# 491 counted edge tiles in place of 363 in a two-layer graph kernel, with the order inside a step changed

## The chip, the cores and the metric

The kernel runs on one core of one Trainium2 chip. The time is device time in microseconds, the median of several runs; a profile shows one execution. The engines are named as in the profile: PE is TensorE (PEld its weight loads), DVE VectorE, ACT ScalarE, POOL GpSimd, SP the engine that issues most plain DMAs.

## The reference

Two graph layers over 12500 nodes of 32 features and 200000 edges, which are sorted by their destination `dst`:

```python
h = jnp.maximum(_layernorm(x, axis=-1), 0.0)
x = x + _L0_gnn_ref(h, L0_gnn_W, L0_gnn_b, src, dst)
h = jnp.maximum(_layernorm(x, axis=-1), 0.0)
x = x + _L1_gnn_ref(h, edge_index, edge_attr_4, W1, b1, W2, b2, W3, b3, W4, b4)
```

The first layer sums over edges and scales by degrees:

```python
out_norm = jax.lax.rsqrt(jnp.maximum(out_deg, 1.0))
in_norm = jax.lax.rsqrt(jnp.maximum(in_deg, 1.0))
h = x * out_norm[:, None]
agg = jax.ops.segment_sum(h[src], dst, num_segments=N_NODES)
out = agg * in_norm[:, None] @ W + b
```

The second makes a message for every edge, `relu` layers of 64, 128 and 64 over `[x_i, x_j - x_i] @ W1`, sums the messages by `dst`, and divides by the in-degree. The edge attributes are not used.

## The kernel before

**Edges.** 1563 tiles (`NTR`) of 128 edges, four tiles to a chunk (391 chunks, `NCH`). Because `dst` is sorted, the edges of a chunk fall into a window of 128 nodes, and the windows of following chunks lie 32 nodes apart. A sum over the edges of a tile is a matmul: the gathered rows as weights, a one-hot of (destination minus window) as the moving operand. Rows are split into three bf16 terms, so that a row has 3 x 32 + 1 columns (`D3` = 97, the last one for the degree).

**First stretch (0 to about 340 us in the profile).** Layer norm of x; out-degrees by one-hot matmuls over all tiles; the table `tab_hn` of scaled rows is written to DRAM. Beside it POOL gathers the unscaled rows of the first 64 chunks (`EARLY`) from `tab_h` and from x, one indirect DMA for a tile of 128 edges (line 211).

**Second stretch (about 340 to 1534 us), the sums of layer 0.** Three kinds of chunks make the sums:

- Early chunks (0 to 63): rows are there already; `scale_rows` finds each edge's factor by a look-up matmul (`look`, line 664) and a mask (line 671), scales the rows (679), splits them into three bf16 terms (copies on ACT, lines 682 and 685; subtractions on DVE, line 687), makes a one-hot (`hot_e`), and sums them (line 693). The generator yields between stages; a new chunk starts at every third step.
- Direct chunks (64 to `DIR` - 1 = 299): POOL gathers their scaled rows from `tab_hn`, four gathers a chunk. `sum_rows` does the matmuls (line 628) into `ps_late`, one PSUM bank, of which four chunks share one group; `add_rows` adds the group to the SBUF sums. Eight buffers hold the gathered rows.
- Counted tiles (all from chunk `DIR` on, `ND` = 363 tiles): nothing is gathered. With source node = 128 x high + low, a tile makes a matrix that counts its edges by (low) x (high, destination in the tile's window of 13): three matmuls (line 775, `count_two` and `count_third`) of a one-hot of low (`lo`) with a one-hot of the key (`oh`, line 713, made for two tiles at once), evicted by two ACT copies (line 777). PSUM has one buffer for each. For a group of eight tiles (`TD`), `multiply` then multiplies the counts by the whole table, held in SBUF, in 98 matmuls (line 724), turns the result (733), places it (743) and adds it (`sums.add`, lines 550 and 552: ACT copies fresh columns, DVE adds to others).

When all chunks that reach a block group of four blocks of 128 nodes (25 groups) are added, `update_nodes` is queued for it: in-degree, W0, residual, layer norm, and two tables, `tab_i` and `tab_j`, written for layer 1. It is a generator in six parts; `in_turn` runs one update at a time, one part for each call.

**The order of work.** The second stretch is one Python loop over chunks, and the engines take their instructions in that order (`manual_schedule`). A step of the loop issues, in this order: the four gathers of chunk m; the one-hot (`hot`) of chunk m + 2; the counting stages due (four stages a tile, spread evenly over the steps); one stage of each running early chunk (`advance`); one part of an update; the start of an early chunk; `add_rows` of chunk m - 3; `sum_rows` of chunk m - 2 (`LAG` = 2). After the loop the rest of the counting and of the updates is issued.

**Third stretch (1534 us to the end), the messages.** POOL gathers rows of `tab_j`, one gather a tile, 1563 in all; it can start when the whole table is written. Four layers and the sums run behind it, and `finish_nodes` writes the output. A last branch handles inputs whose windows do not fit; with these inputs it is not entered.

## Time and profile before

| | us |
|---|---|
| median of 3 runs (3518.82 to 3520.71) | 3519.95 |
| the profiled execution | 3515.0 |
| its span | 3513.1 |
| gathers of the first stretch, 256, first and last start | 6.0, 338.0 |
| row gathers of the second, 944, first and last start | 339.3, 1517.2 |
| gathers of the third, 1563, first and last start | 1534.3, 3484.1 |

The page cuts the span into 40 slices of 87.8 us. A digit is the busy share in tenths, PEclk the granted TensorE clock in tenths; the second stretch is slices 4 to 17:

```profile
PE   3762767777777777547777777777777777777777
...
DVE  8994666556666664213333333333333333333333
ACT  0002555455555555201221222112122121221211
POOL 7777777777777777767777777777777777777775
PEclk9655788778889887658887888887888788887888
```

In rows of groups, the first number after the bar is the busy time of all, the second the mean of one in ns, then the idle time of the engine ahead of them and what ended it. "Issue" is time in which the engine waited for nothing that the profile shows.

### The profile page before, as it was taken

To read this page: it belongs to the slowest core of one execution; us is meant where nothing else is said; L and a number is where in the kernel's file an instruction comes from. 1 tells how busy PE (TensorE), PEld (TensorE's weight loads), DVE (VectorE), ACT (ScalarE), POOL (GpSimd) and SP (SyncE) were. 2 spreads that over 40 slices of the span, in tenths; PEclk is the share of its full clock that TensorE was granted. 3 is DMA by queue.
4 is the path that set the end of the run, shared out by engine and by line. 5 is a ranking of instruction groups with operands and counts; after the bars stand their busy time and mean duration, and the time that the engine had idled before them with its cause. 6 is when DMAs were issued, how large, how long until landed. Compare 5 with 4: busy or idle time off the path is not lost. (4 is left out here: it accounts for less than half of the span.)

```text
span 3513.1 us, 50240 instructions
## 1 busy us (share of the span) xinstructions
PE 2465.8 (70%) x18988; PEld 1733.6 (49%) x18988; DVE 1654.0 (47%) x3694; ACT 1016.1 (29%) x2052; POOL 2622.9 (75%) x2783
## 2 busy tenths in 40 slices
PE   3762767777777777547777777777777777777777
PEld 2650545555555555424445544445544444444445
DVE  8994666556666664213333333333333333333333
ACT  0002555455555555201221222112122121221211
POOL 7777777777777777767777777777777777777775
PEclk9655788778889887658887888887888788887888
DMA  4114111212222211212222222222222222222221
GB/s 94 15 20 72 28 27 30 37 30 38 34 32 36 34 28 30 44 42 59 62 62 61 61 58 61 61 62 58 61 62 61 61 59 61 62 61 61 60 60 31
DMA packets 238466, 173.58 MB, mean 49 GB/s; under 512 B 157810, under 2 KB 186706, under 8 KB 238218
## 3 DMA queue, kind: packets, MB, share of 16 engines
q0 software_dynamic: 88416, 79.14, 14.2%
q1 hardware_dynamic: 131306, 85.26, 8.9%
q10 hardware_dynamic: 18496, 5.89, 1.1%
q8 instruction: 154, 2.52, 0.3%
q14 instruction: 94, 0.77, 0.1%
HBM read 157.16 MB, written 12.92 MB: 48 GB/s over the span
## 5 line engine op out<-in xcount | busy, mean ns | idle before, releaser
L211 POOL DMA_INDIRECT gj<-tab_j,src_j x1563 | 1474.7, 944 | 492.1 <-issue 422.1
L211 POOL DMA_INDIRECT rows<-tab_hn,src_j x944 | 891.5, 944 | 287.7 <-issue 218.8
L916 DVE TENSOR_TENSOR h<-p,b3n 128x512 f32<-128x512 f32 x196 | 135.2, 690 | 731.7 <-PE p L913 731.7
L913 PE MATMUL p<-w3s,h 128*128 128x64 f32 x3128 | 435.5, 298 | 0.3 <-ACT h L905 0.3
L913 PEld LDWEIGHTS p<-w3s,h 128*128 128x128 f32 x3128 | 407.9, 211 | 47.3 <-issue 38.2
L777 ACT ACTIVATE count<-count_two 128x858 bf16<-128x858 f32 x363 | 320.9, 884 | 366.3 <-PE count_two L775 340.1
L881 PE MATMUL p<-gj,ident 128*1 128x8 f32 x392 | 39.1, 175 | 530.1 <-DMA gj<-tab_j,src_j 530.1
L905 ACT ACTIVATE h<-p,b2s 128x1024 f32<-128x1024 f32 x196 | 217.8, 1111 | 641.8 <-PE p L903 641.8
L881 PEld LDWEIGHTS p<-gj,ident 128*1 128x1 f32 x392 | 21.9, 80 | 697.2 <-issue 686.7
L724 PE MATMUL st<-count,table 128*128 128x104 bf16 (+1 forms) x4508 | 333.3, 231 | 35.6 <-ACT count L777 31.9
L931 PEld LDWEIGHTS ps<-hot,h 128*64 128x64 f32 x3126 | 268.9, 188 | 175.0 <-issue 165.3
L724 PEld LDWEIGHTS <-table 128*128 128x128 bf16 x4508 | 304.1, 108 | 103.6 <-issue 67.0
L893 ACT ACTIVATE h<-p 128x512 f32<-128x512 f32 x196 | 117.0, 597 | 810.5 <-PE p L889 810.5
L889 PE MATMUL p<-turned,ai 128*64 128x512 f32 x782 | 327.2, 928 | 0.0
L552 DVE TENSOR_TENSOR acc<-acc,ps 64x64 f32<-64x64 f32 (+1 forms) x198 | 44.7, 226 | 534.1 <-PE ps L931 501.4
L931 PE MATMUL ps<-hot,h 128*64 128x128 f32 x3126 | 293.7, 349 | 0.5 <-DVE h L916 0.5
L775 PE MATMUL count_two<-oh,lo 128*128 128x429 bf16 x726 | 240.5, 418 | 51.6 <-ACT count L777 40.7
L713 DVE TENSOR_TENSOR oh<-keys,kept 128x2574 bf16<-128x2574 f16 x182 | 270.4, 1486 | 13.2 <-PE count_third L775 13.0
L211 POOL DMA_INDIRECT rows_early<-tab_h,src_j x224 | 216.2, 965 | 70.3 <-issue 47.2
L865 DVE TENSOR_TENSOR turned<-row,kept 128x512 f32<-128x512 f16 x391 | 249.4, 678 | 26.9 <-PE p L889 22.1
L575 DVE TENSOR_TENSOR hot<-rel_h,kept 128x512 f32<-128x512 f16 x391 | 249.1, 678 | 0.0
L628 PE MATMUL ps_late<-hot,rows 128*97 128x128 bf16 x944 | 135.0, 254 | 161.9 <-DMA rows<-tab_hn,src_j 89.5
(201 smaller groups left out, 3102.2 us busy)
## 6 DMA issues: line engine op xcount, KB each, us to landing
row<-rel_row SPq DMA_DIRECT2D x195, 256.0 KB
gj<-tab_j,src_j POOLq DMA_INDIRECT x1563
rows<-tab_hn,src_j POOLq DMA_INDIRECT x944
ai<-tab_i SPq DMA_DIRECT2D x195, 64.0 KB
srow<-hi_row SPq DMA_DIRECT2D x64, 98.0 KB
rows_early<-tab_h,src_j POOLq DMA_INDIRECT x224
tab_j<-nu_aij SPq DMA_DIRECT2D x24, 128.0 KB
tab_i<-nu_aij SPq DMA_DIRECT2D x24, 128.0 KB
```

Of the source, the lines that this page charges most:

```text
L211: nc.gpsimd.indirect_dma_start(out=tile_ap, out_offset=None, in_=table, in_offset=bass.IndirectOffsetOnAxis(ap=col, axis=0))
L575: nc.vector.tensor_tensor(hot, rel_h[:, g * TPC : (g + 1) * TPC][:, :, None].to_broadcast([P, TPC, W]), lanes_f[:, None, :W].to_broadcast( ...
L713: nc.vector.tensor_tensor(oh, keys[:, :, i : i + 2][:, :, None, :].to_broadcast([P, 3, KW, 2]), count_h[:, None, :, :].to_broadcast([P, 3, ...
L724: nc.tensor.matmul(ps[:, : tiles * WD], table[:, h, :], c[:, :tiles, h, :], start=(h == 0), stop=(h == PART - 1))
L775: nc.tensor.matmul(ps[:, k, :w], lo[:, i % TPC // 2, :, i % 2], oh[:, k0 + k, :w, i % 2], start=True, stop=True)
L777: nc.scalar.activation(counts[g][:, t, a:b, :].rearrange("p (k h) d -> p k (h d)", k=len(ranges)), ps[:, :, :w], AF.Copy)
L865: nc.vector.tensor_tensor(turned, v["row"][:, k], part_f.to_broadcast([P, CHUNK]), op=OP.is_equal)
L889: nc.tensor.matmul(p1[k * HID : (k + 1) * HID].rearrange("p t e -> p (t e)"), v["ai"][:, k], v["turned"][k], start=False, stop=True, skip_ ...
L905: nc.scalar.activation(h2[:, :n], p2[:, :n], AF.Relu, bias=b2s)
L913: nc.tensor.matmul(p3[:, k * TPC + t, :], v["h2"][:, k, t * P : (t + 1) * P], w3s, start=True, stop=True)
L916: nc.vector.tensor_tensor(h3[:, :n], p3[:, :n], b3n[:, None, :].to_broadcast([P, n, HID]), op=OP.max)
L931: nc.tensor.matmul(ps[k * HID : (k + 1) * HID, o : o + W], v["h3"][:, k * TPC + t, :], v["hot"][k][:, t, :], start=(i == 0 and t == 0), st ...
```

## The change

- `DIR` is 268 in place of 300: 32 chunks (128 tiles) go from the direct to the counted kind. `ND` becomes 491, the groups of eight 62 in place of 46, direct chunks 204 in place of 236.
- `multiply` does its 98 products in 5 stages (n = 8 - 3) in place of 18, and a tile of counting takes one stage in place of three. The last products, the copy `some` and the mask `place` are one stage; the transpose comes in the next, the placing matmul two stages on. A tile is one call of the counting generator in place of four.
- A step has a new order: sums first (early chunks' sums, kept in a list `adds`, and `add_rows`), then a part of an update, then counting, then the stages of early chunks, and `sum_rows` last.
- The early rows are split on DVE alone (`memset`, `tensor_copy`) in place of copies on ACT.
- `hot` has 5 buffers in place of 6, `oh` 4 in place of 3; one-hots are made four tiles ahead in place of two.
- `base`, `base8` and `win_i` move to a pool that is freed after the first stretch.

```diff
-DIR = 300
+DIR = 268
@@ hot_ahead
-            hots[g] = one_hots(sp, rel_h[:, g * TPC : (g + 1) * TPC], W, "hot", AHEAD + 4)
+            hots[g] = one_hots(sp, rel_h[:, g * TPC : (g + 1) * TPC], W, "hot", AHEAD + 3)
@@ scale_rows
-            nc.scalar.activation(rows[:, :, 3 * D :], rows_early[:, g, :, D:], AF.Copy)
+            nc.vector.memset(rows[:, :, 3 * D :], 1.0)
             for k in range(3):
                 part = rows[:, :, k * D : (k + 1) * D]
-                nc.scalar.activation(part, scaled, AF.Copy)
+                nc.vector.tensor_copy(part, scaled)
...
+            adds.append((g, total))
             yield
-            sums.add(slice(0, D3), STEP * g, total)
-            added([g])
@@ onehots_of
-            onehots[i // 2] = oh = dp.tile([P, 3, KW, 2], BF16, name="oh", bufs=3)
+            onehots[i // 2] = oh = dp.tile([P, 3, KW, 2], BF16, name="oh", bufs=4)
@@ multiply
-            n = 3 * TD - 6
+            n = TD - 3
             for s in range(n):
...
-                yield
+                if s < n - 1:
+                    yield
...
             nc.scalar.activation(some[:, : tiles * WD], ps[:D3, : tiles * WD], AF.Copy)
+            width = STEP * (GD - 1) + W
+            place = dp.tile([WD * TD, width], F32, name="place")
+            nc.vector.tensor_scalar(
+                place, count_h[: WD * TD, :width, 0], pos[:, g : g + 1], None, op0=OP.is_equal)
             yield
             ps = pp.tile([P, P + STEP], F32, name="st2")
             nc.tensor.transpose(ps[: WD * TD, :D3], some, ident[:D3, :D3])
             turned = dp.tile([WD * TD, D3], F32, name="some_t")
             nc.scalar.activation(turned, ps[: WD * TD, :D3], AF.Copy)
-            width = STEP * (GD - 1) + W
-            place = dp.tile([WD * TD, width], F32, name="place")
-            nc.vector.tensor_scalar(
-                place, count_h[: WD * TD, :width, 0], pos[:, g : g + 1], None, op0=OP.is_equal)
-            yield
             yield
@@ count_edges
             onehots_of(0)
+            onehots_of(2)
...
-                if i % 2 == 0 and i + 2 < ND:
-                    onehots_of(i + 2)
+                if i % 2 == 0 and i + 4 < ND:
+                    onehots_of(i + 4)
                 oh, lo = onehots[i // 2], los[i // TPC]
-                for _ in range(3):
-                    next(before, None)
-                    yield
+                next(before, None)
@@ the loop
-        steps, stages = DIR - EARLY - 6, 4 * (ND + 2 * TD)
+        steps, stages = DIR - EARLY - 6, ND + 2 * TD
...
             i = m - EARLY
+
+            while adds:
+                early, total = adds.pop()
+                sums.add(slice(0, D3), STEP * early, total)
+                added([early])
+            if EARLY <= m - LAG - 1:
+                add_rows(m - LAG - 1)
+            next(updating)
             for _ in range(stages * i // steps, stages * (i + 1) // steps):
                 next(counting, None)
             advance(running)
-            next(updating)
             later, r = divmod(i, LATER)
             if r == 0 and later < EARLY:
                 running.append(scale_rows(later))
-            if EARLY <= m - LAG - 1:
-                add_rows(m - LAG - 1)
             if EARLY <= m - LAG < DIR:
                 sum_rows(m - LAG)
```

More of the change, by code (lines that the diff above doesn't have):

```diff
@@ L146, in gnn_kernel @@
     pos = early.tile([WD * TD, NDG], F32, name="pos")
-    base = early.tile([1, ND], I32, name="base")
-    base8 = early.tile([TD, NDG], I32, name="base8")
     bounds = early.tile([P, 4], F32, name="bounds")
@@ L154, in gnn_kernel @@
     dst_i = mp.tile([P, NT], I32, name="dst_i")
+    base = mp.tile([1, ND], I32, name="base")
+    base8 = mp.tile([TD, NDG], I32, name="base8")
     first = ctx.enter_context(ExitStack())
@@ L172, in gnn_kernel @@
     nc.gpsimd.iota(lanes_i, pattern=[[1, P]], base=0, channel_multiplier=0)
-    win_i = const.tile([P, NCH], I32, name="win_i")
+    win_i = mp.tile([P, NCH], I32, name="win_i")
     nc.gpsimd.iota(win_i, pattern=[[STEP, NCH]], base=-OFF, channel_multiplier=0)
@@ L594, in gnn_kernel @@
         sums = Sums(np_, D3, "acc", (QE, QD, NQ - 1), (QE, QD), lambda q: ("_e", 2) if q < QE else ("_t", 3) if q < QD else ("_d", 3))
-        hots, rows_of, group_ps, running, updates = {}, {}, {}, [], []
+        hots, rows_of, group_ps, running, updates, adds = {}, {}, {}, [], [], []
         updating = in_turn(updates)
```

## The prediction

> **What bounds the kernel now.** I read the page first, then the kernel in three stretches, then who waits for whom in the middle of the second stretch, then single moments of its timeline.

> ```profile
> span 3513.1 us, 50240 instructions
> PE 2465.8 (70%) x18988; PEld 1733.6 (49%) x18988; DVE 1654.0 (47%) x3694; ACT 1016.1 (29%) x2052; POOL 2622.9 (75%) x2783
> ...
> L211 POOL DMA_INDIRECT gj<-tab_j,src_j x1563 | 1474.7, 944 | 492.1 <-issue 422.1
> L211 POOL DMA_INDIRECT rows<-tab_hn,src_j x944 | 891.5, 944 | 287.7 <-issue 218.8
> ```

> POOL issues 2763 gathers of one edge tile each (1563 + 944 + 224 + 32). One takes 944 ns and the idle time ahead of it is about 0.30 us of plain "issue", so 75% busy is a full queue. By the tile view the 944 row gathers start from 339.3 to 1517.2 us: 1177.9 / 943 = 1.249 us each, 4.996 us for the four of a step. The largest distance between two starts there is 1.36 us, so nothing ever holds POOL in the second stretch. It stands still once only, from the last row gather to the first message gather:

> ```profile
> 1517.22 0.94 POOL L211 DMA_INDIRECT rows<-tab_hn,src_j  x1 [0.30 <-issue]
> ...
> 1519.72 1.82 PEld L474 LDWEIGHTS nu_ps<-w0t,acc 97*128 97x128 f32 x8
> ...
> 1529.71 0.60 ACT L511 ACTIVATE nu_aij<-nu_ps 128x512 f32<-128x512 f32 x1 [2.16 <-PE nu_ps L509]
> ...
> 1534.26 0.94 POOL L211 DMA_INDIRECT gj<-tab_j,src_j  x1 [16.09 <-DMA row<-rel_row]
> ```

> That is 17.0 us: 2.5 us until the last row is in a sum, 10.6 us (1519.7 to 1530.3) for one update of nodes, 4.0 us for its store and the release.

> The other engines have less room than their shares say. This is the view by windows (length, then busy time and instructions of PE, weight loads, DVE, ACT, POOL, the granted clock), and the waits of PE in the same window (total, times, longest), then one of DVE's:

> ```profile
> 600.00:1300.00 700.00, 517.72 (x5232) 398.81 (x5231) 444.04 (x1276) 388.75 (x901) 529.09 (x561) 0.83 0.21 34
> ```

> ```profile
> PE ps_late L628 <- ACT acc_t L550: 49.1, 23, 4.0
> PE st L733 <- ACT some L730: 41.6, 24, 5.2
> PE look L664 <- ACT acc_e L550: 38.7, 39, 2.0
> PE count_two L775 <- ACT count L777: 23.9, 19, 3.9
> PE st L724 <- ACT count L777: 18.1, 22, 2.5
> ...
> PE ps_late L628 <- DMA rows<-tab_hn,src_j: 2.7, 3, 1.1
> ```

> ```profile
> DVE look L687 <- ACT rows_scaled L685: 91.3, 92, 6.1
> ```

> The reader is to see the last PE row: in 700 us PE waited for gathered rows 2.7 us. From each gather's start to the matmul of the same tile it is 2.5 us where PE waits, and 8 to 20 us through most of this window, so PE with its waits needs about the same 5.0 us a step as POOL. The window has 140.1 steps: PE is busy 3.70 us and idle 1.30 us in each, and 129.4 of the 182 idle us (0.92 a step) are three waits on ACT copies that stand behind count evictions.

> **Part by part.** POOL: DIR from 300 to 268 takes away 32 chunks, 128 gathers: 128 x 1.249 = 159.9 us. The last of 816 row gathers would start at 339.3 + 815 x 1.249 = 1357.3 us. The message stretch (1563 gathers) stays.

> Counting: 363 tiles become 491, over 192 steps of the loop in place of 221: 2.56 a step against 1.64, so 0.914 more. At full clock a product group of 16 takes 1.00 us, at half clock 1.55 us:

> ```profile
> 806.02 1.55 PE L724 MATMUL st<-count,table 128*128 128x104 bf16 x16 [2.54 <-ACT count L777]
> ...
> 809.02 1.00 PE L724 MATMUL st<-count,table 128*128 128x104 bf16 x16
> ```

> One tile has 98/8 = 12.25 products: 0.64 us at the 52 ns from start to start, 0.77 us by the row above; its three count matmuls start within 0.57 us (809.86 to 810.43). With its share of transpose and placing, 1.3 to 1.4 us: 1.25 us a step. Today's 3.70 us at a mean clock of 0.83 (0.66 of the time full) is 3.70 x (0.66 + 0.34 x 0.65) = 3.26 us at full clock. New: 4.5 us a step.

> DVE: today 444.0 / 140.1 = 3.17 us a step. A tile adds half an L713 (0.743) and a quarter of a L614 (0.103): 0.77 us a step, placing and sums 0.05. The early chunks' three copies: [...] at most 299 (L687, same shape with two inputs); I take 270. With a memset of 60 to 200 ns, 0.1 taken, it is 0.91 us a chunk, one chunk in three steps: 0.3. Sum 4.3 of 5.0 us. For that L687 no longer waits for ACT, 0.65 us a step of DVE's time.

> ACT: 2.77 us a step, plus 0.914 x (0.884 + 0.513) = 1.28, plus 0.1, less the copies (3 x 0.281 + 0.224) / 3 = 0.36: 3.8 us. Two tiles' evictions back to back start 1.52 us apart (1001.06 and 1002.58), and PSUM has one buffer for them: 2.56 x 1.52 = 3.9 us, under a step.

> The order: with the sums first, the ACT copy that frees ps_late or the look bank is issued ahead of the step's evictions, and PE needs the bank at the step's end; the transpose now comes a whole tile after its copy to "some". All three waits (0.92 us a step) should go. What is late next is PE behind count evictions: L775 and L724 (42 us, 0.30 a step) grow at least with the tiles, and each product group's first matmul needs the last tile's two evictions. I take the remaining 0.38 us of idle times 1.56: 0.6. The bounds are 0.3 (denser filling) and 1.2 (a group start at 1.4 us for each of 62 groups and 0.4 us in each of three tiles of eight without products). The update's stage moves ahead of counting with its matmuls, vector work and, in its last stage, two stores on SP; the early chunk's row load is now queued behind these. A row is needed a step later, so I cost that at nothing[...].

> With hot at 5 buffers, hot for chunk m + 2 waits for the matmul of chunk m - 3, the end of PE's step before. Behind it on DVE are the step's sums, update and one-hots. The one-hots run four tiles ahead (oh at 4 buffers), so PE has its input. Taken at nothing; the slower rival prices it.

> PE's step: if denser work raises the clock to 0.95, 4.5 us take 4.5 / 0.965 = 4.65 us, plus 0.6 = 5.25 us against POOL's 5.0. Counting ends at step 197 of 206, the nine after it hold about 11 us of PE work. PE's end: 197 x 5.25 + 11 = 1045 us against 204 x 4.996 = 1019: 26 us late. POOL may be held a little on the way when its eight row buffers are full; the end is PE's all the same.

> The tail: an update takes six calls, one a step. Following the loop's counters, before, only block group 18 was left when the loop ended. After, groups 3, 4 and 15 come due at steps 194 and 195, group 24 at 196 and group 16 at 206; the loop ends with group 4 at its first stage. So three updates follow the last row: 2 x 10.6 = 21 us more. Cover: none, POOL needs the whole table. The first stretch gets five vector instructions 128 columns longer, under 1 us, hidden by the early gathers. The tiles that change their pool cost nothing.

> Sum: -160 + 21 + 26 = -113 us. Against the profiled execution's 3515.0 that is 3402 us; against the median 3519.95, 3407 us.

> **Rivals.** (1) POOL stays the bound: PE's step at 5.16 us or less, with waits of 0.5 us. For: the three waits were 71% of PE's idle time. Against: PE had no room before. Time 3520 - 160 + 21 = 3381 us. (2) The clock does not rise: 4.5 / 0.88 = 5.1 us plus 0.6 = 5.7 us a step, 115 us late: 3520 - 160 + 21 + 115 = 3496 us. For: PE at 74% busy in the message stretch has 0.82. Against: the gaps that let it fall are the ones that go. (3) Slower: DVE and PE in turn. DVE may start a step only when PE has ended the one before (hot, and the sums that wait for PE's last matmuls); if PE then waits within the step for "place" or for the acc_d sum that frees st, DVE's 4.3 us no longer lie beside PE's. From 5.82 us a step on (0.57 over my 5.25) the gain is gone: (1019 + 139 - 11) / 197. With 0.8 us of such waits a step, 6.05 us: 184 us late, 3565 us. For: DVE at 86%. Against: it works four tiles ahead.

> **Numbers.** Forecast 0.47, POOL bound 0.20, clock 0.18, slower 0.15. The range 3374 to 3506 us holds the first three with about 7 us to spare and leaves the fourth out. No change is what this kernel's runs cannot tell apart, 0.2%, 7 us: faster 0.83, same 0.03, slower 0.14.

> **What would show it.** Right: 816 row gathers, the first message gather near 1420 us, three updates in a row ahead of it, acc_t, "some" and acc_e gone from PE's waits, clock over 0.9 between 350 and 1300, PE waiting mostly for count evictions. Wrong: POOL held by ps_late matmuls for long, PE waiting for DVE within a step, the clock still near 0.83, or PE waiting for rows all along (rival 1).

## The result: 0.3% faster, and the profile after

| | before | after |
|---|---|---|
| median of 8 runs each, us | 3519.36 (3518.17 to 3523.34) | 3509.32 (3508.15 to 3514.82) |
| ratio, 95% interval | | 0.9973 (0.9962 to 0.9984) |
| profiled span, us | 3513.1 | 3508.2 |
| first, last row gather | 339.3, 1517.2 | 338.1, 1489.0 |
| first message gather | 1534.3 | 1525.7 |

The forecast was 3407 us and the range ended at 3506. The kernel is faster, but by 10 us and not by 113. The page of the kernel after:

```profile
span 3508.2 us, 54111 instructions
PE 2569.0 (73%) x20860; PEld 1819.5 (52%) x20860; DVE 1807.6 (52%) x4040; ACT 1140.6 (33%) x2092; POOL 2504.7 (71%) x2655
...
POOL 7777777666665666647777777777777777777775
PEclk9755999889898998857887878888887787878778
...
L211 POOL DMA_INDIRECT rows<-tab_hn,src_j x816 | 771.9, 946 | 380.2 <-issue 203.5
```

POOL's row of tenths is no longer flat: from slice 7 on (the first slice is number 0) it is at 6, once at 5, where it was at 7. The 816 gathers should have taken 816 x 1.249 us; their idle time, 380.2 us, is 131 us over the 0.305 us that each had before (287.7 us for 944). That is where the time went: the last row gather starts at 1489.0 us and not at 1357.3, 131.7 us late. From it to the first message gather it is 36.7 us in place of 17.0. So -159.9 + 131.7 + 19.7 = -8.5 us, which is the difference of the two first message gathers.

The same 600 us window in the middle, by windows (length, busy time and instructions of PE, weight loads, DVE, ACT, POOL, clock), and who waited there (total, times, longest):

```profile
600.00:1200.00 600.00, 472.89 (x5132) 363.36 (x5131) 423.51 (x1149) 371.60 (x726) 382.50 (x405) 0.89 0.18 29
```

```profile
PE count_two L773 <- ACT count L775: 57.4, 73, 3.5
PE st L723 <- ACT count L775: 44.2, 25, 4.5
...
PE st L737 <- ACT some L730: 2.6, 2, 2.3
```

```profile
DVE hot L614 <- PE ps_late L628: 155.9, 58, 5.3
```

The same row in the kernel before, in the 700 us from 600 to 1300 us:

```profile
DVE hot L614 <- PE ps_late L628: 5.8, 9, 1.3
```

And in the kernel after again, from 600 to 1200 us, POOL's wait and the matmuls of the direct chunks (name, count, shortest, median and longest in ns, first and last start):

```profile
POOL rows L211 <- PE ps_late L628: 104.3, 53, 5.1
```

```profile
L628 PE MATMUL ps_late<-hot,rows x396: 217/218/314, 600.0 to 1197.5; 128*97 128x128 bf16 x198
```

396 matmuls are the chunks of 99 steps, so a step of PE takes 6.06 us. (POOL's 405 gathers are 101 steps: it runs ahead of PE as far as its eight row buffers go, so gathers do not count PE's steps.) PE is busy 4.78 us of a step, where 4.65 was forecast, and idle 1.28 us, where 0.6 was forecast. The three waits that the new order was to remove are gone (ps_late and look on ACT; "some" from 41.6 us of 700 to 2.6 of 600). In their place PE waits for count evictions, 101.6 us (42.0 of 700 before); POOL waits for the row buffers that PE has not read; and DVE has one wait that it hardly had before, 155.9 us, or about 1.6 us a step, at the one-hot that opens each step.

The chain from that wait to PE can be read at a single moment of the timeline (start, length, instruction, idle time ahead of it and what ended it; a few rows are left out):

```profile
908.58 0.40 PE L628 MATMUL ps_late<-hot,rows 128*97 128x128 bf16 x4
...
909.01 0.42 DVE L614 TENSOR_TENSOR hot<-rel_h,kept 128x512 bf16<-128x512 f16 x1 [2.86 <-PE ps_late L628]
...
909.82 0.55 PE L773 MATMUL count_two<-oh,lo 128*128 128x429 bf16 x2
...
910.84 0.29 DVE L492 TENSOR_TENSOR nu_h<-x,nu_m 128x128 f32<-128x128 f32 x1
911.16 0.31 ACT L493 ACTIVATE nu_t<-nu_h 128x128 f32<-128x128 f32 x1 [1.98 <-DVE nu_h L492]
...
912.09 0.20 ACT L496 ACTIVATE nu_g<-nu_m 128x4 f32<-128x4 f32 x1 [0.62 <-DVE nu_m L495]
912.20 0.87 ACT L775 ACTIVATE count<-count_two 128x858 bf16<-128x858 f32 x1
...
913.12 0.55 PE L773 MATMUL count_two<-oh,lo 128*128 128x429 bf16 x2 [1.51 <-ACT count L775]
```

At 908.58 PE does the last matmuls of a step. DVE has stood still 2.86 us for them, because its next instruction is the one-hot, whose buffer they free. Behind it in DVE's queue is the update's arithmetic, to 911.1; ACT's square (L493) waits 1.98 us for that; and the eviction of counts that PE had ready at 910.4 stands in ACT's queue behind the square and behind a second small instruction of the update (L496), which waits 0.62 us for DVE in its turn, until 912.20. PE, with one PSUM buffer for the counts, then waits 1.51 us. In the whole window PE waits for DVE directly hardly at all: the rows of PE's waits that name DVE come to 4.3 us of 127.

### The profile page after: what moved, and what is told of

It is laid out like the page before. It is cut to its first block, busy times and chain, and to the rows that moved or that the text cites. A ratio compares the mean times of both kernels' runs of the same rounds, so it can differ in the third digit from the quotient of the medians.

```text
span 3508.2 us, 54111 instructions
## 1 busy us (share of the span) xinstructions
PE 2569.0 (73%) x20860; PEld 1819.5 (52%) x20860; DVE 1807.6 (52%) x4040; ACT 1140.6 (33%) x2092; POOL 2504.7 (71%) x2655
## 5 line engine op out<-in xcount | busy, mean ns | idle before, releaser
L211 POOL DMA_INDIRECT gj<-tab_j,src_j x1563 | 1478.0, 946 | 512.0 <-issue 423.8
L211 POOL DMA_INDIRECT rows<-tab_hn,src_j x816 | 771.9, 946 | 380.2 <-issue 203.5
L775 ACT ACTIVATE count<-count_two 128x858 bf16<-128x858 f32 x491 | 434.5, 885 | 261.2 <-PE count_two L773 230.1
L723 PE MATMUL st<-count,table 128*128 128x104 bf16 (+1 forms) x6076 | 393.4, 223 | 67.2 <-ACT count L775 64.6
L723 PEld LDWEIGHTS <-table 128*128 128x128 bf16 x6076 | 367.4, 103 | 116.4 <-issue 48.3
L773 PE MATMUL count_two<-oh,lo 128*128 128x429 bf16 x982 | 294.7, 384 | 128.3 <-ACT count L775 118.2
L712 DVE TENSOR_TENSOR oh<-keys,kept 128x2574 bf16<-128x2574 f16 x246 | 364.9, 1487 | 3.6 <-PE count_third L773 3.6
L211 POOL DMA_INDIRECT rows_early<-tab_h,src_j x224 | 215.6, 963 | 71.5 <-issue 49.4
L773 PEld LDWEIGHTS <-lo 128*128 128x128 bf16 x1473 | 140.5, 105 | 222.9 <-issue 169.2
L775 ACT ACTIVATE count<-count_third 128x416 bf16<-128x416 f32 x491 | 251.6, 512 | 0.0
```

Of the source, the lines that this page charges most:

```text
L211: nc.gpsimd.indirect_dma_start(out=tile_ap, out_offset=None, in_=table, in_offset=bass.IndirectOffsetOnAxis(ap=col, axis=0))
L712: nc.vector.tensor_tensor(oh, keys[:, :, i : i + 2][:, :, None, :].to_broadcast([P, 3, KW, 2]), count_h[:, None, :, :].to_broadcast([P, 3, ...
L723: nc.tensor.matmul(ps[:, : tiles * WD], table[:, h, :], c[:, :tiles, h, :], start=(h == 0), stop=(h == PART - 1))
L773: nc.tensor.matmul(ps[:, k, :w], lo[:, i % TPC // 2, :, i % 2], oh[:, k0 + k, :w, i % 2], start=True, stop=True)
L775: nc.scalar.activation(counts[g][:, t, a:b, :].rearrange("p (k h) d -> p k (h d)", k=len(ranges)), ps[:, :, :w], AF.Copy)
```

## Experiments

Two theories for the 1.28 us of idle time. **H**: the wait of the one-hot holds DVE, DVE's work behind it holds ACT, ACT's evictions hold PE. **E**: the two evictions and their one PSUM buffer are the pace, whatever DVE does. **U**, a part of H: the place of the update ahead of counting is the cost. Ratios are against the kernel before, run beside each. The expectations count steps by POOL's gathers (1.26 us idle, 1.54 us of waiting and 5.95 us a step in the changed kernel); the steps of PE given here are counted by its matmuls of line 628.

**1. The one-hot made for one chunk ahead in place of two, same five buffers.** The buffer that it takes is then one whose matmuls are a step older.

```diff
-            for g in range(m, m + AHEAD + 1) if m == EARLY else [m + AHEAD]:
+            for g in range(m, m + AHEAD) if m == EARLY else [m + AHEAD - 1]:
```

> The one-hot of a direct chunk is made one chunk ahead in place of two, with the same five buffers, so DVE needs the matmuls of two steps ago and not those of the step just before. Theory H (the wait of the one-hot holds DVE at the start of each step, DVE's update and sums then hold ACT's copies, and the count evictions queued behind these hold PE): DVE's 1.54 us a step of waiting for ps_late goes, PE's idle time falls from 1.26 to about 0.7 us a step, the step from 5.95 to about 5.3 us, the time to about 3400 us. Theory E (the two evictions of a tile and the one PSUM buffer they empty set the pace, whatever DVE does): no change, 3509 us within 8, the wait only moves to another DVE instruction.

Measured 3420.91 us, ratio 0.9738 (0.9722 to 0.9754). The window, DVE's largest waits and PE's two largest in this run:

```profile
600.00:1200.00 600.00, 490.30 (x5607) 378.44 (x5606) 468.03 (x1265) 404.36 (x796) 427.58 (x453) 0.94 0.20 33
```

```profile
DVE acc_e L552 <- PE look L693: 50.6, 26, 4.5
DVE acc_t L552 <- PE ps_late L628: 29.3, 15, 3.9
...
DVE hot L614 <- PE ps_late L628: 1.9, 1, 1.9
```

```profile
PE count_two L773 <- ACT count L775: 55.9, 85, 3.2
PE st L723 <- ACT count L775: 42.8, 31, 4.0
```

The window has 432 matmuls of line 628, 108 steps of 5.56 us; PE is busy 4.54 and idle 1.02 us of each. The one-hot's wait falls from 155.9 to 1.9 us, and ACT's waits for DVE from 82 to 47 us of the window. The clock rises from 0.89 to 0.94, and 83 us (by the two ratios) to 88 us (by the two medians) of time go. H holds, with a gain somewhat smaller than it said; E, which said no change, falls. But count evictions are still what PE waits for most, 0.91 us a step after 1.03. What is left of DVE's waiting is in the sums.

The whole second stretch, from the first row gather to the first message gather, by windows, shows how the gain is made up. First the changed kernel, then this run:

```profile
338.10:1525.70 1187.60, 926.88 (x10052) 711.54 (x10051) 841.59 (x2315) 723.89 (x1417) 771.91 (x816) 0.88 0.18 30
```

```profile
338.40:1437.00 1098.60, 883.25 (x10052) 680.10 (x10051) 840.87 (x2314) 716.66 (x1416) 771.02 (x817) 0.93 0.20 33
```

The stretch is 89.0 us shorter. PE's idle time falls by 45.4 us of that; the other 43.6 us are busy time, of the same 10052 matmuls at a mean clock of 0.93 in place of 0.88. (An estimate from the prediction's two product groups, 1.55 us at half clock and 1.00 us at full clock, with the mean clock read as a share of time as there, gives about 892 us of busy time at 0.93; it is 883.)

**2. The waiting instruction last in the step, nothing else.** Here the one-hot of chunk m + 2 keeps its buffers and the matmuls that it needs; its place in the queue changes: the three lines of `hot_ahead` go to the end of the loop's body.

> The changed kernel with the one-hot of chunk m + 2 issued as the last instruction of the step and not as its first, again, where the kernel before takes 3512 to 3520 us. Five buffers, the lead and the wait (the matmuls of chunk m - 3) stay; only what is queued behind it on DVE changes. Theory H: as the earlier one-hot, ratio about 0.974, DVE's wait for ps_late at the one-hot under 20 us of 600. If the gain came from the extra step of buffering: DVE still waits, ratio 0.99 or more.

Measured 3420.21 us, ratio 0.9734 (0.9717 to 0.9750). DVE in this run:

```profile
DVE acc_e L552 <- PE look L693: 50.8, 26, 4.5
DVE acc_t L552 <- PE ps_late L628: 29.4, 15, 3.9
...
DVE hot L614 <- PE ps_late L628: 2.0, 1, 2.0
```

The same time and the same waits as in experiment 1, because it is the same order of work. The end of step m and the start of step m + 1 are one place in DVE's queue, and there both kernels make the one-hot of chunk m + 2. In the two traces PE, ACT and POOL have the same instructions in the same order, and DVE too but for two one-hots in the first step. So this run repeats experiment 1 on another chip; it could not tell the step's work behind the one-hot from the extra step of buffering, as the expectation meant it to. Both runs show that five buffers are enough if the one-hot comes a step later. That it can wait at no cost is not shown, since it no longer waits; and six buffers at the old place were not run.

**3. The update back behind counting.**

```diff
-            next(updating)
             for _ in range(stages * i // steps, stages * (i + 1) // steps):
                 next(counting, None)
             advance(running)
+            next(updating)
```

> The part of an update goes back behind the counting and the early chunks of its step; sums stay first. Theory H: the evictions no longer stand behind the update's ACT instructions (about 30 of 84 us in which ACT waits for DVE between 600 and 1200 us), but still behind the sums that wait for DVE: a part of the gain, 3460 to 3490 us. Theory U (the place of the update alone is the cost): most of the 105 us, about 3410 us. Theory E: no change.

Measured 3498.54 us, ratio 0.9957 (0.9941 to 0.9974). This missed H's figure of 3460 to 3490 and rules out U, which said about 3410: the interval overlaps that of the changed kernel (0.9962 to 0.9984). DVE's wait at the one-hot stays (155.3 us), and ACT's waits for DVE do not fall. Those in the update's square (21.0 us before this edit) and in two of the sums (16.4 and 11.8 us) are all longer:

```profile
ACT nu_t L493 <- DVE nu_h L492: 30.6, 8, 4.5
ACT acc_t L550 <- DVE acc_t L552: 24.7, 16, 4.0
ACT acc_e L550 <- DVE acc_e L552: 20.8, 22, 2.3
```

**4. The early rows split on ACT again**, `nc.scalar.activation` for the memset and the three copies.

> The early rows are split by ACT copies again, as before the change. Theory H: DVE has 0.3 us a step less to do but waits for ACT between the copies; 0 to 60 us slower than the changed kernel, 3510 to 3570 us. If DVE's own work (4.19 us busy a step) were what sets the pace: faster, 3450 us or so.

Measured 3529.05 us, ratio 1.0045 (1.0028 to 1.0062), about 20 us above the changed kernel, although DVE has 0.3 us a step less to do (388.3 us for 97 steps of the window, against 423.5 us for 99). The split on DVE is worth its price. Its price, in the tile view of the changed kernel:

```profile
L685 DVE CAST rows_scaled<-look x192: 293/294/296, 355.8 to 1461.4; 128x128 bf16<-128x128 f32 x192
...
L682 DVE MEMSET rows_scaled<- x64: 62/62/62, 355.8 to 1460.0; 128x4 bf16 x64
```

**5. The old order with 491 tiles:** the kernel before with `DIR = 268` and the three tiles in the other pool.

> The kernel before with DIR = 268 and the three tiles in the other pool, nothing else: 491 counted tiles in the old order of a step, products in 18 stages, split on ACT. If the new order gives what it was taken to give: PE's step is 5.0 us plus 0.914 tiles at 1.4 us plus their waits, 6.4 to 6.6 us, some 285 us late, 3600 to 3660 us. If the new order brings nothing because another wait took the place of those removed: 3509 us, as the changed kernel.

Measured 3630.29 us, ratio 1.0335 (1.0318 to 1.0353); 364 gathers and as many matmuls in the window, 6.59 us a step. The waits that the new order removes are all there:

```profile
PE st L733 <- ACT some L730: 38.2, 27, 2.7
...
PE ps_late L628 <- ACT acc_t L550: 29.7, 15, 3.6
...
PE look L664 <- ACT acc_e L550: 24.0, 27, 1.4
```

So the new order, stages, split and buffers together are worth about 125 us at 491 tiles as they stand, and about 210 with the one-hot out of the way.

**6. The new order with 363 tiles**, the changed kernel with `DIR = 300`.

> The changed kernel with 363 counted tiles, again. PE's step under POOL's 5.0 us: POOL sets the time, within 7 us of the kernel before. If the held one-hot costs PE more than 0.3 us a step at 363 tiles too: above before, ratio 1.002 to 1.01, and POOL held by ps_late matmuls.

Measured 3513.73 us, ratio 1.0004 (0.9995 to 1.0012): no change. DVE waits as long at the one-hot as with 491 tiles, and it costs nothing, because PE now waits for POOL:

```profile
PE ps_late L628 <- DMA rows<-tab_hn,src_j: 45.8, 54, 3.4
```

```profile
DVE hot L614 <- PE ps_late L628: 155.2, 66, 5.6
```

**7. The sums behind the first counted tile** (in place of ahead of the update), with the one-hot of experiment 1.

```diff
             next(updating)
-            for _ in range(stages * i // steps, stages * (i + 1) // steps):
-                next(counting, None)
+            for k in range(max(1, stages * (i + 1) // steps - stages * i // steps)):
+                if k < stages * (i + 1) // steps - stages * i // steps:
+                    next(counting, None)
+                if k == 0:
+...
```

> The kernel with the one-hot one chunk ahead and the sums behind the first counted tile, again, where the kernel before takes 3512 to 3520 us. Theory H: 20 to 35 us below the 3421 us of the one-hot alone, about 3390 us, ratio to before 0.965. Theory E: ratio 0.974, no change to the one-hot alone.

Measured 3397.93 us, ratio 0.9671 (0.9655 to 0.9688), 23 us under experiment 1; 444 matmuls of line 628 in the window, 5.41 us a step after 5.56. DVE's waits in the sums fall from 79.9 (acc_e and acc_t in experiment 1) to 50.2 us. That is what H forecast for the same link in the sums.

**8. Two parts of updates a step at the end**, with the edits of 1 and 7: `for _ in range(1 if i < steps - 4 else 2): next(updating)`.

> One-hot one chunk ahead, sums behind the first counted tile, and two parts of updates a step in the last 13 steps, so that one update and not three follows the last row. Against the run with the first two edits: 21 us less, if an update alone costs 10.6 us in the tail; about 3370 us. If the doubled parts hold PE up in the last steps: 10 us less or nothing.

Measured 3387.76 us, ratio 0.9645 (0.9629 to 0.9661), the fastest kernel of the study, 125 us under the kernel before. The step from experiment 7 is 10 us, not 21, the second case of the expectation: from the last row gather to the first message gather it is 30.5 us (39.6 in 7). PE ends the last rows' sums 9.4 us after that gather starts, where in the kernel before it was 2.5 us, and two updates, not one, are finished after them. What exactly makes it late there was not tried.

**On two other chips** the same kernels ran with a kernel before of 4374 and 4343 us. Experiments 7, 6 and 2 ran there first: ratios 0.9960 (0.9944 to 0.9976), 1.0064 (1.0043 to 1.0084) and 0.9994 (0.9977 to 1.0011). Two more ran only there:

> One-hot one chunk ahead, and in the last 13 steps two parts of updates a step, so that one update is left behind the last gathered row and not three. If an update alone costs 10.6 us in the tail, as the profile of before shows for one: 21 us less than 3421, 3400 us, and the gap between the last row gather and the first message gather falls from 37.7 to about 17 us. If updates overlap in the tail: less, 3410 us or so.

> One-hot one chunk ahead, and the part of an update behind counting and the early chunks. Theory H: with DVE freed the place of the update matters little, 3421 us within 10. Theory U (the update ahead of counting costs in its own right): 15 us less or more, as the same edit alone brought 10 to 15 us.

The first (experiment 1 and the doubled parts) gave 4381.51 us, ratio 1.0017 (1.0007 to 1.0027); the second (experiment 1 and the late update) 4368.49 us, ratio 0.9991 (0.9979 to 1.0002). The gains that were forecast did not come on those chips, where the best of the five runs is 0.4% faster. They do not decide between the theories: a message gather takes about 1.46 us there (481 in the 700 us from 2500 us on, in the run of experiment 2) in place of 1.25, in the message stretch that no edit touches, so something else holds the kernel. Whether the late update adds anything to the earlier one-hot is open.

## Why the prediction was wrong

- **What bounds the kernel, the 160 us of POOL, the first stretch:** right. The 128 gathers are gone, and nothing came back ahead of the second stretch.
- **PE's work:** right, 4.78 us a step for 4.65 at a clock of 0.89, and 4.54 in experiment 1 at 0.94, near the 0.95 that was taken. **ACT's** 3.75 (3.8) and **DVE's** 4.28 (4.3) too. The copies took 294 ns (L685), where 270 was taken: the trace of before has no such copy, and the 270, below the 299 of L687, was the author's estimate alone. The memset took 62 ns, where 0.1 us was taken.
- **The three waits of PE on ACT copies:** right, gone, and experiment 5 shows what they would have cost.
- **The tail:** right, three updates, 36.7 us for 38.2.

```profile
1489.03 0.94 POOL L211 DMA_INDIRECT rows<-tab_hn,src_j  x1 [0.30 <-issue]
...
1501.59 0.60 ACT L511 ACTIVATE nu_aij<-nu_ps 128x512 f32<-128x512 f32 x1 [2.16 <-PE nu_ps L509]
...
1510.69 0.49 ACT L511 ACTIVATE nu_aij<-nu_ps 128x384 f32<-128x384 f32 x1 [1.74 <-PE nu_ps L509]
...
1521.19 0.60 ACT L511 ACTIVATE nu_aij<-nu_ps 128x512 f32<-128x512 f32 x1 [2.16 <-PE nu_ps L509]
...
1525.75 0.94 POOL L211 DMA_INDIRECT gj<-tab_j,src_j  x1 [35.77 <-DVE turned L868]
```

The last copy of each of the three updates is here (the rows of line 511), 9.1 to 10.5 us apart.

- **The step that failed:** hot at five buffers: "The one-hots run four tiles ahead (oh at 4 buffers), so PE has its input. Taken at nothing". The wait and the queue behind it were named; the question of who waits for that queue was asked of PE alone. ACT waits for it: the sums and the update have ACT instructions that follow DVE ones, and the change had put both, on ACT too, ahead of the count evictions. So DVE's delay reaches PE through ACT, and four tiles of one-hots do not help. Size, by the prediction's own sum of 197 steps and 11 us: PE's row matmuls run from 340.6 to 1491.6 us, which makes a step of 5.79 us; in experiment 1 from 340.9 to 1402.1, which makes 5.33. In place of nothing the held one-hot cost 0.46 us a step, some 85 to 90 us of time. Experiment 1 shows this, and 2 repeats it. The road through ACT is read from the traces: ACT's waits for DVE fall by 35 us of 600 in experiment 1, and nearly all of PE's waits are for ACT. No run changed that road alone.
- **PE's other waits:** 0.6 us a step was taken; with the one-hot out of the way 1.02 were left in the window, and over the stretch 26 us late became 42. Part of the excess is the same link in the sums (experiment 7 took 0.15 us a step). The bound of 1.2 us that the prediction set from above was passed in the changed kernel (1.28); the two terms given for it come to only 0.84 us a step. The forecast's own case, a PE step of 5.25 us and 3407 us, is near what experiment 1 measured by the same sum: 5.33 us and 3421.
- **The clock:** 0.89 for a taken 0.95; it is 0.94 in experiment 1, where only the order of work differs, so it came with that order and was no cause of its own. But up to half of the held one-hot's cost is PE's busy time, which fell as the clock rose (43.6 of 89.0 us; some 35 of these by the estimate in experiment 1). The prediction's reading of the clock comes out of the trace of before, from 340 to 1517 us, in windows of 3.41 us: of 57 half-clock windows followed by a full-clock one, PE was busy for over 80% in 56, and all 43 full-clock windows with PE busy for less than half were followed by a half-clock one; so were 14 in which it was busy for more. In the kernel after, between 340 and 1489 us, 45 full-clock windows were followed by a half-clock one, and in 42 of them PE was busy for less than half of the window. Rival 2's number, 3496 us, came nearest, but by luck: its PE busy time of 5.1 us a step and its idle time of 0.6 are both wrong.
- **The rivals:** by mechanism the third was nearest. It named the place and a decision point of 5.82 us a step; by the same sum the change came out at 5.79 and ended 10 us ahead. (By that sum, rival 1 needed 5.12 us and not 5.16.) Its road was wrong in the main: "place" cost PE 2.0 us in 600, the evictions 101.6. But the acc_d sum that it named stands in the chain: from 662 to 666 us PE's weight load waits 3.24 us for it, ACT's copy beside it 3.32 us, and the count eviction that PE needs is queued behind that copy until 665.69.

## What to carry to other kernels

Of an instruction that waits at the start of a step ask not only who needs its result, but who needs what is queued behind it, through each engine's queue in turn; here a one-hot at the start of DVE's step, which had to wait for its buffer, cost some 85 to 90 us, and five buffers were enough once it stood at the step's end, where it hardly had to wait. Reordering and more work must be judged together: the reordered kernel without more counting brought nothing (ratio 1.0004), the counting alone cost 3.4%, both with the one-hot moved gave 2.7% (0.9734). Where an engine falls short of its rate, look for the wait on another engine that grew, here DVE's 155.9 us of 600 after 5.8 of 700, and see whether moving the waiting instruction removes it. And count an engine's steps by its own instructions: POOL's gathers, ahead of PE by up to eight buffers, made PE's step look 0.1 to 0.3 us shorter.

## What was not expected

Two of the five chips of the experiments ran these kernels, the one before included, at 4340 to 4400 us, a quarter longer. Instructions took as long there (in the run of experiment 7 on such a chip, from 1000 to 1012 us, a row gather 0.94 to 0.95 us and the eviction of 858 columns 0.88 to 0.89 us; 0.95 and 0.89 in the changed kernel), but much of the engines' standing still ends in no release that the trace ties to a wait. ACT and PE in the window from 600 to 1200 us of the run of experiment 2 on such a chip ("remote" is a release from a source outside the trace, "issue" none at all):

```profile
ACT count L775 <- remote: 88.5, 24, 7.6
```

```profile
PE st L723 <- issue: 20.3, 30, 1.2
```

No run here shows the cause. An edit worth 2.7% on one chip was worth nothing on such a one (0.9994), so the ratios above stand only for chips on which the kernel before takes the same time.
